# Two small transfers per attention job begun from ScalarE's queue instead of SyncE's, in a two-layer transformer kernel

## The chip, the cores and the metric

The kernel runs on one core of one Trainium2 chip. The time is device microseconds (us) of one execution of the whole program, and of several runs the median is taken. Engines are named as in the profile: PE is TensorE (PEld its weight loads), ACT is ScalarE, DVE is VectorE, POOL is GpSimd and SP is SyncE. SP does no arithmetic in this kernel: it begins the transfers.

## The reference

The input `x` has shape (2, 1024, 1024) in float32. Four blocks follow one another, each of the form `x = x + block(layernorm(x))`:

1. causal attention with rotary positions, 32 query heads and 8 key/value heads of width 32, over 2 sequences of 1024 tokens;
2. a mixing block: per token a 4x4 matrix made doubly stochastic in 50 Sinkhorn iterations, which mixes four streams of 256 columns, and one small matmul branch;
3. a second causal attention of the same sizes with the other pairing of the rotary columns;
4. a linear layer of 1024 by 1024 with a bias plus a mixture of eight rank-16 adapters, whose weights come from a softmax gate and a threshold.

For the change only the attention matters. For one group of 4 query heads that share a key head:

```python
scores = q @ k.T / sqrt(32)          # masked above the diagonal
attn = softmax(scores, axis=-1)      # minus the row's maximum inside the exponential
out = attn @ v
```

## The kernel before

**Tiles and stages.** Tokens are taken in blocks of 512. Matmuls are done in three passes on pairs of a high and a low part (`PASSES`), so that float32 accuracy is kept. The plan `P0 P1 O0 M0 P2 O1 ...` (`PLAN`) orders the dense work of both layers: P projects a block to queries, keys and values, O is the output projection, M the logits of the mixing block, F the last linear layer with its mixture. Beside it run the attention jobs: 8 blocks by 8 key heads are 64 jobs (`JOBS`), counted here from 0 to 63. PE's work is dealt out from six streams: results, values, branches, scores, maxima and the dense rest.

**One attention job.** `load_job` brings keys into a tile `kst` and the four heads' queries into a tile `qst` (rows 0 to 95 of its partitions; three of each rotate). Then come three passes over the same scores:

- `maxima_of` computes the scores with queries on the partitions (L1002). DVE takes the row's maximum, with its sign turned, into a column of `nm` (L1012), and ACT makes the sum of the exponentials (L1027, an ACTIVATE and a read of its accumulator). That is 16 rows of tiles per job. At the end PE transposes `nm` into a bank (L1039), and DVE writes the transposed row of maxima into `lt` as a high part (`lt[:, 0]`, L1045) and a low part (`lt[:, 1]`, L1050).
- Two small transfers (L1055 to L1063) copy `lt[:, 0]` and `lt[:, 1]`, 8 KB each, into partitions 96 and 97 of `qst`. Rows 96 and 97 of `kst` hold ones, so the next matmul subtracts the maxima by itself.
- `scores_of` computes the scores again, with keys on the partitions and these two more rows (L1091). ACT takes the exponential out of the bank into `pt` (L1098), POOL masks the diagonal (L1108), and `values_of` multiplies by the values (L1154).

The event `summed[j]` stands for the landing of both small transfers, and the first matmul of L1091 of job j waits for it.

**What sets the order.** Nothing is ordered by the compiler: a planner written in the kernel (`Planner`) plays the program through with costs for every operation and writes the instructions out in the order in which it begins them. An operation's `fn` is called at its planned beginning. So each engine runs its own instructions in that order, and the places of instructions of different engines in the one written list tell what the planner held to be simultaneous. Transfers are planned by `pl.dma` on SP: 430 ns of SP for each, and eight "lanes" in turn: a transfer waits until the transfer eight before it in the list has landed, since both count on one semaphore. Which engine really begins a transfer is decided by what `fn` calls: everywhere in this kernel `nc.sync.dma_start`. The planner's cost for a transfer stays with SP whatever `fn` calls.

An engine's queue is strictly in order. An instruction that waits for a semaphore holds up all that stand behind it on the same engine.

Of the kernel before, what the change touches and what calls it, by code (L numbers as in the profile page):

```python
# [66 lines left out]
def fp(ap):  # L67
    return ap.bitcast(FP)
# [3 lines left out]
def t_act(n, sbuf=False, accum=False):  # L72
    ns = n / 1.2 + (95.0 if sbuf else 66.0)
    if accum:
        ns += 170.0
    return max(ns, 95.0), max(ns, 95.0) + 105.0


def t_dve(n):
    return n / 0.96 + 67.0, n / 0.96 + 150.0  # L80
# [15 lines left out]
def t_pe(n):  # L96

    return max(n, 256) * 0.4531 + 2.0
# [408 lines left out]
def kernel(ctx: ExitStack, tc: tile.TileContext, a: dict, out: bass.AP):  # L507
    nc = tc.nc
# [469 lines left out]
    def maxima():  # L978
        for j, (n, g) in enumerate(JOBS):
            yield from maxima_of(j, n, g)  # L980

    def maxima_of(j, n, g):

        half = n % 2
        kt, qt, _, there, _ = loaded[j]


        npc = half + 1
        nm, nm_was, nm_rel = nm_ring.take()
        ds, ds_was, ds_rel = ds_ring.take()  # L990
        found, sums = [], []
        for i in range(TPB):
            N = (half * TPB + i + 1) * P // npc
            M = max(N, 256)
            for r in (0, 2, 1, 3):
                col = slice(r * 4 + i, r * 4 + i + 1)
                ms, ms_was, ms_rel = ms_ring.take()
                ev = None
                for p in range(npc):

                    def go(bk, r=r, i=i, p=p):
                        nc.tensor.matmul(  # L1002
                            bk[:, :M], qt[0:96, r, i * P : (i + 1) * P],
                            kt[0:96, p * N : p * N + M], start=True, stop=True,
                        )

                    end, bank = yield Step(
                        [there], t_pe(M), go, bank=True, quota=of_sums
                    )

                    def least(sc=bank.tile[:, :N], col=col, N=N, p=p, ms=ms):
                        nc.vector.tensor_tensor_reduce(  # L1012
                            out=ms[:, p * N : (p + 1) * N], in0=sc,
                            in1=cmask[:, TB - N :] if p == half else zero.to_broadcast([P, N]), scale=1.0,
                            scalar=nm[:, 1, col] if p else MASKED,
                            op0=ALU.add, op1=ALU.min, accum_out=nm[:, int(p < half), col],
                        )

                    ev = pl.dve(
                        (N / 0.96 + 142.0, N / 0.96 + 225.0), least,  # L1020
                        [end, nm_was, ms_was] + ([ev] if ev else []), PRI_SUMS,
                    )
                    bank.free.follow(ev)
                found.append(ev)
                ev = pl.act(
                    t_act(npc * N, True, accum=True),
                    lambda ms=ms, col=col, N=N: nc.scalar.activation(  # L1027
                        ms[:, : npc * N], ms[:, : npc * N], AF.Exp, bias=nm[:, 0, col], scale=-1.0,
                        accum_out=ds[:, col],
                    ),  # L1030
                    [ev, ds_was], PRI_DEN,
                )
                ms_rel.follow(ev)
                sums.append(ev)

        ev = pl.dve((175.0, 265.0), lambda ds=ds: nc.vector.reciprocal(ds, ds), sums)
        dens[j] = (ds, ev, ds_rel)
        end, bank = yield Step(
            found, T_TURN, lambda bk, nm=nm: nc.tensor.transpose(bk[:16, :P], nm[:, 0], ident), bank=True  # L1039
        )  # L1040
        nm_rel.follow(end, *sums)
        lt, was, rel = lt_ring.take()
        tp = bank.tile[:16, :P]
        ev = pl.dve(
            t_dve(P), lambda lt=lt, tp=tp: nc.vector.tensor_scalar(lt[:, 0], tp, -1.0, None, ALU.mult),  # L1045
            [end, was], PRI_SUMS,
        )
        ev = pl.dve(
            t_dve(P),
            lambda lt=lt, tp=tp: nc.vector.scalar_tensor_tensor(  # L1050
                lt[:, 1], tp, -1.0, fp(lt[:, 0]), ALU.mult, ALU.subtract
            ), [ev], PRI_SUMS,
        )
        bank.free.follow(ev)
        evs = [  # L1055
            pl.dma(
                512,
                lambda q=q, qt=qt, lt=lt: nc.sync.dma_start(
                    fp(qt[96 + q : 97 + q]).rearrange("k r q -> k (r q)"), fp(lt[:, q])
                ), 16, [ev], -2,  # L1060
            )
            for q in range(2)
        ]  # L1063
        rel.follow(*evs)
        summed[j].follow(*evs)
# [873 lines left out]
```

## Time and profile before

| what | value |
|---|---|
| three runs of the kernel | 2308.69, 2311.53, 2321.01 us; median 2311.53 |
| the profiled execution | 2316.82 us, of which its span (first to last instruction) is 2315.1 us |
| granted TensorE clock | 0.991 of full speed |
| PE, DVE, ACT, POOL busy | 97%, 79%, 73%, 43% of the span |
| instructions that ACT executes | 4062 |
| transfers begun by SP | 1363, of which 128 are those of the change |

How to read the profile: "busy" is the time in which an engine executes; waiting, and the beginning of a transfer, are not counted. The ends of matmuls are modelled, so a busy PE can still be held up a little. "SPq" is SyncE's sequencer, which begins transfers. In a line of the timeline the columns are start in us, duration in us, engine, line of the program, operation, output<-inputs with their shapes and a count; brackets show idle time of the engine just before and what ended it. In a line of waits the columns are who waited for whom, the total in us, how often, and the longest.

### The profile page before, as it was taken

How to read it: one execution, taken by the hardware profiler on the slowest of the kernel's cores; microseconds unless marked ns; L12 is line 12 of the kernel's file. 1: busy time of each engine (PE TensorE's matmuls, PEld its weight loads, DVE VectorE, ACT ScalarE, POOL GpSimd, SP SyncE). 2: the span in 40 equal slices, each digit the busy share in tenths (PEclk: the TensorE clock that was granted, in tenths of full speed). 3: DMA queues.
4: the chain of work that ended last, by engine and by line, in shares of the span. 5: the costliest groups of instructions: out<-in, count | busy, mean ns of one | idle time of the engine just before them, and what ended most of it. 6: DMA issues, size and time to landing. Idle time of an engine off the chain costs nothing.

```text
span 2315.1 us, 42175 instructions
## 1 busy us (share of the span) xinstructions
PE 2244.4 (97%) x12544; PEld 1639.6 (71%) x12544; DVE 1834.3 (79%) x5826; ACT 1697.5 (73%) x4062; POOL 992.3 (43%) x1438
## 2 busy tenths in 40 slices
PE   9999999999999999999999999999999999999999
PEld 8767856666676766667776676668777766666787
DVE  7767979998898999988899989978875887656253
ACT  4798769999574899999978867862894697558320
POOL 5444424555456654325763345643443423212100
PEclk9999999999999999999999999999999999999999
DMA  8866554447667655438683565448857826453554
GB/s 295 275 182 216 198 173 138 141 134 238 211 214 242 210 160 189 141 102 271 191 260 112 170 224 184 142 167 288 287 164 247 274 83 223 132 184 94 209 190 146
DMA packets 217750, 445.69 MB, mean 193 GB/s; under 512 B 55984, under 2 KB 66480, under 8 KB 211376
## 3 DMA queue, kind: packets, MB, share of 16 engines
q1 hardware_dynamic: 217520, 442.99, 59.1%
q8 instruction: 99, 1.62, 0.3%
q14 instruction: 131, 1.07, 0.1%
HBM read 308.16 MB, written 133.69 MB: 191 GB/s over the span
## 4 chain that ended last, share of the span: by engine, by line
PE 73%; DVE 10%; DMA 9%; ACT 4%; issue 2%; POOL 1%; SPq 1%; DVEq 0%; POOLq 0%; ACTq 0%
PE bank L859 16%; PE bank L1275 13%; PE bank L1002 11%; PE bank L1091 9%; PE bank L1154 9%; PE bank L1716 8%; DVE ms L1012 3%; PE bank L816 3%; DMA qst<-qd 2%; ACT ms L1027 2%; ACT pt L1098 2%; DMA qst<-lt 1%; PE bank L783 1%; DMA x<-x 1%; DVE stat L737 1%
## 5 line engine op out<-in xcount | busy, mean ns | idle before, releaser
L1027 ACT ACTIVATE ms<-ms,nm 128x128 f32<-128x128 f32 (+5 forms) x1024 | 802.4, 791 | 77.0 <-DVE nm L1012 74.8
L1098 ACT ACTIVATE pt<-bank 128x512 f32<-128x512 f32 (+1 forms) x1216 | 657.6, 592 | 98.6 <-PE bank L1091 95.2
L1002 PE MATMUL bank<-kst,qst 96*128 96x384 f32 (+4 forms) x1536 | 494.2, 367 | 23.1 <-DMA qst<-qd 15.6
L859 PE MATMUL bank<-zT,w 128*128 128x512 f32 x1920 | 504.6, 397 | 0.0
L1091 PE MATMUL bank<-qst,kst 98*128 98x512 f32 (+1 forms) x1216 | 430.6, 400 | 17.9 <-DMA qst<-lt 8.6
L1275 PE MATMUL bank<-w,zT 128*128 128x512 f32 x1536 | 413.6, 398 | 4.8 <-DMA zT<-od 2.2
L859 PEld LDWEIGHTS bank<-zT,w 128*128 128x128 f32 x1920 | 354.9, 189 | 81.5 <-issue 8.6
L1002 PEld LDWEIGHTS bank<-kst,qst 96*128 96x128 f32 x1536 | 276.2, 191 | 180.9 <-DVE nm L1012 34.5
L1108 POOL TENSOR_SCALAR_AFFINE_SELECT pt<-pt 128x256 f32<-128x256 f32 (+1 forms) x448 | 208.5, 469 | 369.6 <-ACT pt L1098 364.5
L1012 DVE CUSTOM_DVE_ANT_0 ms<-bank,cmask,nm 128x448 f32<-128x448 f32 (+3 forms) x512 | 316.9, 628 | 29.5 <-PE bank L1002 12.8
L1275 PEld LDWEIGHTS bank<-w,zT 128*128 128x128 f32 x1536 | 284.7, 189 | 66.8 <-issue 4.9
L1012 DVE CUSTOM_DVE_ANT_0 ms<-bank,zero 128x448 f32<-128x448 f32 (+3 forms) x512 | 292.6, 577 | 45.8 <-PE bank L1002 33.8
L1154 PE MATMUL bank<-pt,vst 128*32 128x512 f32 (+3 forms) x3072 | 315.5, 497 | 2.9 <-POOL pt L1108 1.6
L1091 PEld LDWEIGHTS bank<-qst,kst 98*128 98x128 f32 x1216 | 224.5, 190 | 96.4 <-issue 23.9
L660 POOL TENSOR_TENSOR w<-rw,w 128x512 fp32r<-128x512 f32 x169 | 224.7, 1330 | 150.8 <-ACT w L651 119.8
L1012 DVE CUSTOM_DVE_ANT_0 ms<-bank,cmask 128x384 f32<-128x384 f32 (+3 forms) x512 | 234.4, 480 | 51.6 <-ACT ms L1027 34.1
L651 ACT CAST w<-rw 128x512 fp32r<-128x512 f32 x156 | 97.1, 623 | 182.0 <-DMA rw<-in_w 69.9
L1027 ACT ACTIVATION_READ_ACCUMULATOR ms<-ms,nm 128x1 f32 x1024 | 216.9, 212 | 0.0
L1716 PE MATMUL bank<-w,zT 128*128 128x512 f32 x768 | 194.9, 398 | 0.0
L1154 PEld LDWEIGHTS bank<-pt,vst 128*32 128x32 f32 x3072 | 76.6, 108 | 134.2 <-issue 86.2
L1716 PEld LDWEIGHTS bank<-w,zT 128*128 128x128 f32 x768 | 143.6, 189 | 37.1 <-issue 4.8
L659 DVE TENSOR_TENSOR w<-rw,w 128x512 fp32r<-128x512 f32 x77 | 61.9, 804 | 85.0 <-ACT w L651 82.0
(171 smaller groups left out, 2812.7 us busy)
## 6 DMA issues: line engine op xcount, KB each, us to landing
rw<-in_w SPq DMA_DIRECT2D x246, 256.0 KB, 3.3
w<-wd SPq DMA_DIRECT2D x114, 512.0 KB, 4.3
x<-x SPq DMA_DIRECT2D x72, 512.0 KB, 5.0
qd<-st SPq DMA_DIRECT2D x64, 512.0 KB, 4.3
qst<-qd SPq DMA_DIRECT2D x64, 512.0 KB, 5.9
od<-st SPq DMA_DIRECT2D x63, 512.0 KB, 3.6
zT<-od SPq DMA_DIRECT2D x63, 512.0 KB, 8.1
wd<-w SPq DMA_DIRECT2D x38, 512.0 KB, 4.0
```

What stands on the lines that cost most here:

```text
L651: (ACT, t_act(512, True), lambda: nc.scalar.copy(me.tile[:, 0], raw)),
L660: (GPS, t_gtt(512), lambda: nc.gpsimd.tensor_tensor(me.tile[:, 1], raw, fp(me.tile[:, 0]), ALU.subtract), True),
L859: nc.tensor.matmul(ps, w.tile[:, i, (c % 4) * P : (c % 4 + 1) * P], zT[:, j, c, :], start=(c == 0 and m == 0), stop=(c == NC - 1 and m == 2),)
L1002: nc.tensor.matmul(bk[:, :M], qt[0:96, r, i * P : (i + 1) * P], kt[0:96, p * N : p * N + M], start=True, stop=True,)
L1012: nc.vector.tensor_tensor_reduce(out=ms[:, p * N : (p + 1) * N], in0=sc, in1=cmask[:, TB - N :] if p == half else zero.to_broadcast([P, N] ...
L1027: lambda ms=ms, col=col, N=N: nc.scalar.activation(ms[:, : npc * N], ms[:, : npc * N], AF.Exp, bias=nm[:, 0, col], scale=-1.0, accum_out=d ...
L1091: nc.tensor.matmul(to, ks, qs, start=True, stop=True)
L1098: lambda to=pt[:, r : r + nm], st=bank.tile, nm=nm, W=W: nc.scalar.activation(to, st[:, : nm * W].rearrange("p (r t) -> p r t", r=nm), AF. ...
L1108: lambda pt=pt, nh=nh: nc.gpsimd.affine_select(out=pt[:, :, :P], in_=pt[:, :, :P], compare_op=ALU.is_ge, fill=0.0, base=0, pattern=[[0, nh ...
L1154: nc.tensor.matmul(to[HD * r : HD * r + HD, q0:], vt[:, kb, :], pts[r * len(pts) // 4][0][:, r % (4 // len(pts)), :], start=(kb == 0), sto ...
L1275: nc.tensor.matmul(ps, zT[:, x, c, i * P : (i + 1) * P], ws[c].tile[:, y, :], start=(c == 0 and m == 0), stop=(c == NC - 1 and m == 2),)
L1716: nc.tensor.matmul(ps, x_, w_, start=(c == 0 and m == 0), stop=(c == NC and m == 2))
```

## The change

The two small transfers of the row of maxima are begun by ACT on its own queue, `nc.scalar.dma_start` in place of `nc.sync.dma_start`. The planner is not told: it goes on planning them on SP, so the written list keeps its order, and no other instruction is added, removed or moved.

```diff
@@ -1055,7 +1055,7 @@
         evs = [
             pl.dma(
                 512,
-                lambda q=q, qt=qt, lt=lt: nc.sync.dma_start(
+                lambda q=q, qt=qt, lt=lt: nc.scalar.dma_start(
                     fp(qt[96 + q : 97 + q]).rearrange("k r q -> k (r q)"), fp(lt[:, q])
                 ), 16, [ev], -2,
             )
```

## The prediction

> **What bounds the kernel now.** I read the page first, then the waits, the view of the tile `lt`, the chain, and the timeline around single jobs.
>
> ```profile
> PE 2244.4 (97%) x12544; PEld 1639.6 (71%) x12544; DVE 1834.3 (79%) x5826; ACT 1697.5 (73%) x4062; POOL 992.3 (43%) x1438
> ...
> PE 73%; DVE 10%; DMA 9%; ACT 4%; issue 2%; POOL 1%; SPq 1%; DVEq 0%; POOLq 0%; ACTq 0%
> ```
>
> PE is busy nearly throughout: only 2315.1 - 2244.4 = 70.7 us of the span are PE idle, and all that the change could win on PE is among them. ACT's 73% is a mean, and the stretches differ:
>
> ```profile
> 410.00:550.00 140.00, 140.00 (x806) 93.91 (x805) 127.19 (x470) 135.09 (x324) 81.84 (x141) 1.00 0.45 142
> 550.00:660.00 110.00, 105.28 (x617) 77.94 (x616) 94.19 (x259) 73.78 (x209) 50.11 (x62) 1.00 0.79 262
> ```
>
> After the stretch and its length stand PE, PEld, DVE and ACT busy. From 410 to 550 us ACT is busy 135 of 140 us; from 550 to 660 only 74 of 110. New work on ACT is nearly free in the second and not in the first. Of the small transfers the view of `lt` and the waits say:
>
> ```profile
> L1058 SPq DMA_DIRECT2D qst<-lt x128: 503/525/1861, 85.0 to 2121.8; - x128
> ...
> DMA to landing us min/median/max: 1.8/2.9/11.8
> ```
>
> ```profile
> PE bank L1002 <- DMA qst<-qd: 15.6, 8, 4.0
> PE bank L1091 <- DMA qst<-lt: 8.6, 6, 2.8
> ...
> PE bank L1091 <- ACT pt L1098: 4.4, 8, 1.2
> ```
>
> SP spends 525 ns (median) beginning one; it lands 1.8 to 11.8 us later. PE idles for them 8.6 us in all, in 6 jobs of 64; all 8.6 us may be won, hardly more.
>
> **Removed from SP.** 128 beginnings of 0.525 us, 67 us of SP, and the waits for DVE ahead of them. That matters where a transfer right behind them ends on the chain. I went through the six transfers behind each pair: of the 33 transfers on the chain six stand there, in an unbroken row (the first after job 7, 27, 46, 53, 55, 58). Each can start up to 1.05 us sooner: 0 to -6.3 us. I take **-3**.
>
> **Added to ACT: the beginnings.** 128 x 0.525 = 67.2 us, 1.05 us a job, as no row shows a transfer begun by ACT. From below: semaphore instructions on ACT's sequencer take 17 ns (rows of L1027) and end, in the median, 0.34 us before the end of an ACTIVATE in front of them, so the sequencer runs ahead and may hide part. Behind a read of the accumulator, which most of the 64 places follow, they end with it, so there it hides nothing. From above: 1.86 us each, SP's maximum. I take 0.85 us a job, near the 1.05 of SP's rows, with 0.4 and 1.05 as ends.
>
> How much reaches PE? In the written list I took the place of each pair, and from the ACT instruction behind it followed the recorded waits (ACT's own order, ACT to DVE, POOL and PE, with some 35 to 75 ns per hand-over) to the first matmul; the smallest sum of the gaps is how late ACT may be there without PE being late. The easiest place to read is job 29:
>
> ```profile
> 952.21 1.16 SPq L1058 DMA_DIRECT2D qst<-lt  x2
> ...
> 953.66 0.29 ACT L1027 ACTIVATION_READ_ACCUMULATOR ms<-ms,nm 128x1 f32 x1
> 953.75 0.96 ACT L1098 ACTIVATE pt<-bank 128x384 f32<-128x384 f32 x2
> ...
> 954.38 0.19 PEld L1091 LDWEIGHTS bank<-qst,kst 98*128 98x128 f32 x1
> 954.47 0.35 PE L1091 MATMUL bank<-qst,kst 98*128 98x384 f32 x1
> ```
>
> SP begins at 952.21. ACT reaches the place, between the two ACT rows, at 953.95; then comes the exponential, whose first half ends at 954.33, and PE's next weights load at 954.38, 0.05 us later, into the bank it empties. The allowance is zero; 0.85 us there is 0.85 us for PE. In job 61 the allowance is 7 us. Over 64 jobs, 38 have less than 0.85 us; the shortfalls sum to **24.2 us** (8.4 us at a delay of 0.4, 32.0 at 1.05).
>
> **Added to ACT: waits.** The pair now waits on ACT for `lt` (DVE L1045, L1050) and for the landing of the transfer eight before. Against ACT's recorded arrival DVE is mostly done (median 0.7 us earlier) and the lane free. Exceptions, such as jobs 43 (4.1 us, lane), 1 (1.7), 56 (2.1) and 20 (1.4), sum to 13.1 us. Behind the waiting transfer stand the exponentials of L1027 and L1098, for which DVE (`ms`), POOL (`pt`) and PE (banks) wait. The share that passes on I take as above, 24.2 of 54.4: **+5.8**.
>
> Both make 30 us. PE's other idle time, 70.7 - 8.6 = 62 us or 1 us a job, is partly spent waiting for things that ACT doesn't delay, and eats some lateness. I take off a fifth: **+24**.
>
> **Moved: when the pair lands.** The second is begun 1.25 us later than on SP (mean over jobs: ACT arrives later, and in 45 jobs has one to six instructions between the two). Yet a transfer on ACT's queue doesn't stand behind SP's. In the trace 24 of 64 land in under 1.9 us, and those behind a backlog take longest, as job 56's second:
>
> ```profile
> 1828.28 4.02 SPq L1255 DMA_DIRECT2D zT<-od  x7
> ...
> 1835.65 2.30 SPq L1058 DMA_DIRECT2D qst<-lt  x2
> ```
>
> Behind seven loads of 512 KB it took 10.4 us. At 1.8 us throughout, PE saves 8.9 us of its gaps and is late by 2.7 in ten jobs (-6.2). At 2.9, now's median, it saves 8.4 and loses 20.0 (+11.6). Some sharing remains; I take 2.1 us: 8.9 saved, 5.8 lost, **-3**.
>
> [...]
>
> **Sum.** -3 + 24 - 3 = +18 us. Against the profiled execution that is 2316.8 + 18 = 2335 us; that run lay 5.3 us above the median of three, so against the median 2311.5 + 18, rounded to **2330 us**. 0.5% is 11.6 us, about what a measurement of this kernel can tell from no change.
>
> **Rivals.**
>
> *It is hidden (about 2313).* The sequencer runs ahead and ACT loses 0.4 us a job: 8.4 + 3 for waits, less 6.2 for landing at 1.8 us and 3 for SP, +2. For it: ACT's median of 0.34 us ahead, and that PE idles for ACT only 4.4 us now. Against it: PE's weight loads do wait for ACT, 22.0 us in 32 cases (L1002) and 20.4 in 46 (L1091).
>
> *Faster (about 2297): the transfers leave SP's backlog.* The chain runs through `qst<-lt` five times (6.9, 5.3, 3.1, 3.4, 10.4: 29.1 us). At 1.8 us each, 20 us go; SP's part gives 6 more; less 8.4 + 3 on ACT, -15. It decides if ACT loses under some 0.4 us a job and landing takes 1.8 us. Against it: PE's idle before those matmuls is 8.6 us, so not all 20 can come out.
>
> *ACT becomes the bound (about 2385).* All 67 us plus 13 us of waits pass on, less 6 as above. For it: long rows without ACT gaps, such as 1891 to 1907 us. Against it: ACT idles 27% overall.
>
> *It does not do what it says:* ACT's transfers land as slowly as SP's; then the landing term is +11.6 and the time 2344, within the forecast's range.
>
> **How the numbers follow.** Forecast (2316 to 2350) 0.50, of which 0.37 lies over 0.5% slower and 0.13 within; hidden 0.20, of which 0.17 within and 0.03 slower; faster 0.18; ACT the bound 0.12. So faster 0.18, same 0.17 + 0.13 = 0.30, slower 0.37 + 0.03 + 0.12 = 0.52. The range from 2299 to 2368 leaves out about half of the faster case (0.09) and most of the last (0.09).
>
> **What would show it.** Beginnings: rows of L1058 on ACT, near 0.5 us, ACT idle before the instruction behind them. Passing on: PEld waits for ACT (L1002, L1091) above 22.0 and 20.4 us, PE idle above 70.7. Landing: a median near 2.1 us and the 8.6 us wait of L1091 nearly gone. I am wrong if ACT's rows of L1058 are far from 0.5 us, if PE's idle time doesn't grow, or if most new PE idle is behind transfers that SP begins.

## The result and the profile after

The changed kernel takes 2335.49 us (median of 6 runs, 2331.26 to 2347.62), the kernel before in the same setting 2312.67 us (6 runs, 2307.27 to 2321.01). The ratio is 1.0104, with a 95% interval from 1.0082 to 1.0125: about 24 us slower. The profiled execution of the changed kernel took 2336.56 us with a span of 2334.8 us, 19.7 us more than that of before.

The same two lines of the page as shown of before, busy times and the chain, now read:

```profile
PE 2253.0 (96%) x12544; PEld 1639.3 (70%) x12544; DVE 1831.5 (78%) x5826; ACT 1697.8 (73%) x4062; POOL 996.5 (43%) x1438
...
PE 75%; DMA 9%; DVE 8%; ACT 3%; issue 2%; POOL 1%; SPq 1%; ACTq 0%; DVEq 0%; POOLq 0%
```

PE is idle for 2334.8 - 2253.0 = 81.8 us instead of 70.7, which is 11.1 of the 19.7 us. The other 8.6 us are matmuls that took longer. ACT's busy time has not moved (1697.8 us against 1697.5), since beginning a transfer isn't counted as busy. The tile `lt`, again with the rows that answer to those of before:

```profile
L1058 ACTq DMA_DIRECT2D qst<-lt x128: 510/516/1583, 82.7 to 2139.6; - x128
...
DMA to landing us min/median/max: 1.8/2.7/7.9
```

A beginning on ACT takes 516 ns in the median, as on SP (525), and the landing takes 2.7 us, hardly less than 2.9. PE's waits, columns as before:

```profile
PE bank L1002 <- DMA qst<-qd: 10.7, 5, 4.0
PE bank L1002 <- DVE nm L1012: 9.9, 12, 3.0
PE bank L1091 <- DVE nm L1012: 5.9, 9, 1.8
PE bank L1002 <- ACT rd L1222: 5.2, 1, 5.2
PE bank L1091 <- ACT pt L1098: 4.6, 8, 1.4
...
PE bank L1091 <- DMA qst<-lt: 3.3, 3, 1.4
```

The two rows of before on DVE's maxima (`nm`):

```profile
PE bank L1002 <- DVE nm L1012: 4.6, 7, 1.4
...
PE bank L1091 <- DVE nm L1012: 1.9, 5, 0.7
```

The wait for the pair itself is nearly gone (8.6 to 3.3 us). What is new is PE waiting for DVE's maxima (4.6 to 9.9 us at L1002, 1.9 to 5.9 at L1091) and one wait of 5.2 us for ACT's `rd`. DVE did not become slower (1831.5 us busy, 1834.3 before). It was held up by ACT, as ACT's own waits say:

```profile
ACT ms L1027 <- DMA od<-st: 7.2, 2, 3.7
...
ACT ms L1027 <- DMA zT<-od: 5.7, 2, 4.3
ACT rd L1222 <- DMA kst<-kd: 5.6, 1, 5.6
ACT ms L1027 <- DMA qst<-qd: 5.0, 1, 5.0
```

None of these four lines exists before. They look absurd: the sum of exponentials at L1027 has nothing to do with the output `od`, with its reload `zT` or with another job's queries. The timeline resolves it. Here is ACT at job 56:

```profile
1848.09 0.83 ACT L1027 ACTIVATE ms<-ms,nm 128x640 f32<-128x640 f32 x1
1848.82 0.19 ACT L1027 ACTIVATION_READ_ACCUMULATOR ms<-ms,nm 128x1 f32 x1
1852.65 0.52 ACTq L1058 DMA_DIRECT2D qst<-lt  x1
1853.27 0.83 ACT L1027 ACTIVATE ms<-ms,nm 128x640 f32<-128x640 f32 x1 [4.26 <-DMA zT<-od]
...
1859.43 0.52 ACTq L1058 DMA_DIRECT2D qst<-lt  x1
1860.05 0.83 ACT L1027 ACTIVATE ms<-ms,nm 128x640 f32<-128x640 f32 x1 [5.04 <-DMA qst<-qd]
```

ACT stands still from 1849.01 to 1852.65 although DVE had written the first half of `lt` by 1846.00, and starts nothing that stands behind the small transfer; in both traces its 4062 instructions start in the same order. The waiting instruction is the small transfer, and it waits for its lane: the transfer eight before it in the list has to land, since both count on one semaphore. For the first that is the sixth of seven loads `zT<-od` of 512 KB (begun 1843.68, landed 1852.63), for the second a load `qst<-qd` (begun 1847.22, landed 1859.41); each of the two begins 0.02 us after that landing. SP had only just begun them, behind megabytes of other loads (the first row holds the last five of the seven loads):

```profile
1842.15 3.21 SPq L1255 DMA_DIRECT2D zT<-od  x5
...
1847.22 0.50 SPq L952 DMA_DIRECT2D qst<-qd  x1
```

Such stalls stand in four jobs: 5.57 us in job 1, 1.39 and 3.56 in job 18, 3.68 and 1.67 in job 43, 4.26 and 5.04 in job 56, **25.2 us of ACT's time in all**. Of these, 20.7 us are the wait for the lane. The other 4.5 us are the seven beginnings behind these waits: there ACT has nothing left to do, so a beginning stands in the open, some 0.6 us each up to ACT's next row (1852.65 to 1853.27). I compared matmul by matmul when PE starts it after and before. PE falls behind by 6.25 us from 550 to 660 us (job 18), 7.4 from 1320 to 1430 (job 43) and 5.6 from 1760 to 1880 (job 56), together 19.2 of the 19.7 us. Job 1 leaves 1.5 us, because PE's old wait of 2.85 us for its pair goes. What the other stretches add and give back nearly cancels.

**Why these places.** With all transfers on SP, the eighth before a transfer is also eight back in SP's own queue, usually long landed (for the small transfers in the trace of before, 9.4 us earlier in the median, under 0.1 us earlier for 8 of the 128). Once two engines begin transfers, the lanes are still dealt in the one written list into which the framework merges all engines: in the trace of after ACT's 128 transfers count on the same eight semaphores as SP's 1235. The planner's list kept its order; this merged list did not, which the semaphores of the transfers' landings show. In it the pair now stands later among SP's transfers than it did: by 3 and 3 places in job 1, by 2 and 5 in job 18, by 6 and 7 in job 43, by 3 and 6 in job 56, and by none for 87 of the 128. "Eight before" then means one that SP began a few us ago. The ACT instructions behind the pair make `ms`, whose tiles DVE needs back for L1012, and PE waits for DVE: that is the chain behind the lines above.

### The profile page after: what moved, and what is told of

Read it like the earlier page. It is cut to its first block, busy times and chain, and to the rows that moved or that the text cites. A ratio compares the mean times of both kernels' runs of the same rounds, so it can differ in the third digit from the quotient of the medians.

```text
span 2334.8 us, 42125 instructions
## 1 busy us (share of the span) xinstructions
PE 2253.0 (96%) x12544; PEld 1639.3 (70%) x12544; DVE 1831.5 (78%) x5826; ACT 1697.8 (73%) x4062; POOL 996.5 (43%) x1438
## 4 chain that ended last, share of the span: by engine, by line
PE 75%; DMA 9%; DVE 8%; ACT 3%; issue 2%; POOL 1%; SPq 1%; ACTq 0%; DVEq 0%; POOLq 0%
PE bank L859 17%; PE bank L1275 13%; PE bank L1002 11%; PE bank L1091 9%; PE bank L1154 9%; PE bank L1716 8%; DMA qst<-qd 3%; PE bank L816 3%; DVE ms L1012 2%; DMA x<-x 1%; ACT pt L1098 1%; DVE stat L737 1%; PE bank L783 1%; ACT ms L1027 1%; DMA zT<-od 1%
## 5 line engine op out<-in xcount | busy, mean ns | idle before, releaser
L1027 ACT ACTIVATE ms<-ms,nm 128x128 f32<-128x128 f32 (+5 forms) x1024 | 801.7, 790 | 93.4 <-DVE nm L1012 70.9
L1098 ACT ACTIVATE pt<-bank 128x512 f32<-128x512 f32 (+1 forms) x1216 | 657.8, 591 | 96.5 <-PE bank L1091 91.3
L1002 PE MATMUL bank<-kst,qst 96*128 96x384 f32 (+4 forms) x1536 | 498.0, 369 | 30.8 <-DMA qst<-qd 10.7
L1091 PE MATMUL bank<-qst,kst 98*128 98x512 f32 (+1 forms) x1216 | 432.8, 401 | 20.4 <-DVE nm L1012 5.9
L1002 PEld LDWEIGHTS bank<-kst,qst 96*128 96x128 f32 x1536 | 276.8, 191 | 194.5 <-DVE nm L1012 44.3
L859 PEld LDWEIGHTS bank<-zT,w 128*128 128x128 f32 x1920 | 354.8, 189 | 81.8 <-issue 8.6
L1012 DVE CUSTOM_DVE_ANT_0 ms<-bank,cmask,nm 128x448 f32<-128x448 f32 (+3 forms) x512 | 317.1, 629 | 25.7 <-PE bank L1002 9.3
L1012 DVE CUSTOM_DVE_ANT_0 ms<-bank,zero 128x448 f32<-128x448 f32 (+3 forms) x512 | 293.0, 578 | 53.1 <-PE bank L1002 28.0
L1091 PEld LDWEIGHTS bank<-qst,kst 98*128 98x128 f32 x1216 | 225.7, 191 | 101.8 <-ACT pt L1098 21.0
L1012 DVE CUSTOM_DVE_ANT_0 ms<-bank,cmask 128x384 f32<-128x384 f32 (+3 forms) x512 | 234.6, 480 | 57.9 <-ACT ms L1027 39.4
L1027 ACT ACTIVATION_READ_ACCUMULATOR ms<-ms,nm 128x1 f32 x1024 | 215.5, 210 | 0.0
```

What stands on the lines that cost most here:

```text
L859: nc.tensor.matmul(ps, w.tile[:, i, (c % 4) * P : (c % 4 + 1) * P], zT[:, j, c, :], start=(c == 0 and m == 0), stop=(c == NC - 1 and m == 2),)
L1002: nc.tensor.matmul(bk[:, :M], qt[0:96, r, i * P : (i + 1) * P], kt[0:96, p * N : p * N + M], start=True, stop=True,)
L1012: nc.vector.tensor_tensor_reduce(out=ms[:, p * N : (p + 1) * N], in0=sc, in1=cmask[:, TB - N :] if p == half else zero.to_broadcast([P, N] ...
L1027: lambda ms=ms, col=col, N=N: nc.scalar.activation(ms[:, : npc * N], ms[:, : npc * N], AF.Exp, bias=nm[:, 0, col], scale=-1.0, accum_out=d ...
L1091: nc.tensor.matmul(to, ks, qs, start=True, stop=True)
L1098: lambda to=pt[:, r : r + nm], st=bank.tile, nm=nm, W=W: nc.scalar.activation(to, st[:, : nm * W].rearrange("p (r t) -> p r t", r=nm), AF. ...
```

## The experiments

Each was timed in several rounds beside the kernel before on the same chip. That kernel's median differs between chips (2313.1, 2317.6 and 2317.9 us in the three groups of runs), so ratios are compared; a difference in us is the ratio times the median of its group. Each profile is of one execution, which can lie up to some 11 us from its kernel's median (e4: 2325.2 against 2336.7 us).

**1 and 2. The four jobs alone, and all others.** In e1 the pairs of jobs 1, 18, 43 and 56 go back to SP, all others stay on ACT:

```diff
-                lambda q=q, qt=qt, lt=lt: nc.scalar.dma_start(
+                lambda q=q, qt=qt, lt=lt, j=j: (nc.sync if j in (1, 18, 43, 56) else nc.scalar).dma_start(
```

In e2 the two engines in that line are exchanged, so that only those four are on ACT.

> The pairs of jobs 1, 18, 43 and 56 are begun by SyncE as before, the other 60 pairs by ScalarE. Theory 'lane' (ScalarE loses its time in these four jobs, where it waits for the landing of a transfer of SyncE that counts on the same semaphore): the loss is gone, within 5 us of the kernel before, ScalarE idle at the 60 places about as long as before. Rival 'issue' (the recorded prediction's main term: 0.5 us of ScalarE for each beginning, spread over some 38 jobs): 60 of 64 pairs keep their cost, +21 us. Rival 'late landing' (the second transfer of every pair begins later): +15 to +20 us.

> Only the pairs of jobs 1, 18, 43 and 56 are begun by ScalarE, the other 60 by SyncE. 'Lane': most of the change's loss, +14 to +22 us, with ScalarE idle 3 to 6 us at these places and TensorE idle there. 'Issue': 8 beginnings of 0.5 us, at most +4 us. 'Late landing': +1 to +2 us.

e1: ratio 1.0026 [1.0006, 1.0047], or +6.0 us for 60 jobs. e2: 1.0069 [1.0047, 1.0092], or +16.0 us for 4 jobs. For e1 that is a little outside the 5 us of 'lane', but far from the 15 to 21 us of the rivals; e2 is as 'lane' said. The two add up to 22 of the 24 us. So 120 of the 128 moved transfers cost about a quarter of the loss and 8 cost two thirds. In e2's profile PE falls behind by 5.75, 5.76 and 5.60 us in the stretches of jobs 18, 43 and 56, and ACT's four odd waits are all there; in e1's they are gone.

**3 and 5. The other merge.** A switch of the framework's context decides how the engines' lists are merged into the one in which lanes are dealt. Each engine's own order is the same in both. With the other rule, the pairs of those four jobs stand no later among SP's transfers than before. (In e3 some pairs of other jobs stand up to four places later, but ACT shows no long wait there: L1027, L1098 and L1222 wait for transfers once, 1.2 us. By this, a later place cost ACT time only in the four jobs, where SP had a backlog.) e3 has all 64 pairs on ACT, e5 only the four.

```diff
-    with tile.TileContext(nc, schedule_with_timeline_sim=True) as tc:
+    with tile.TileContext(nc, schedule_with_timeline_sim=False) as tc:
```

> All 64 pairs on ScalarE as in the change, every engine's order unchanged; only the order in which the engines' instructions are merged into one list differs, and with it which transfer stands eight before each one, that is which landing a transfer waits for. The four jobs' pairs no longer have a transfer that SyncE has only just begun as their predecessor, some twenty other second transfers have one that is two to four places younger. 'Lane': most of the loss goes, 0 to +9 us. 'Issue' and 'late landing': unchanged, +20 to +25 us.

> Only the pairs of jobs 1, 18, 43 and 56 are begun by ACT, and the written list is merged by the other rule, under which every engine keeps its order and no pair is dealt a later lane. Theory 'lane' (the loss is ACT's wait for a transfer that SP has only just begun): the 18.6 us that these four jobs cost under the first merge are gone; between -7 us (jobs 1 and 56 no longer stand behind SP's backlog) and +2 us against before, and no ACT idle time above 1 us behind a transfer of these four jobs. Rival 'issue' (each beginning costs ACT its 0.5 us): +1.5 us, and it cannot be told from the lane theory by the time alone, but then ACT's instruction behind each pair starts some 0.5 to 1 us later than in before. Rival 'the place': in these four jobs any transfer begun by ACT is dear, whatever lane it has: +15 to +19 us, as with these four under the first merge.

e3: 1.0000 [0.9979, 1.0020]. The whole loss of the change is gone with all 128 transfers still on ACT. e5: 0.9971 [0.9955, 0.9988], 6.7 us *faster* than before, where the same four jobs under the first merge cost 16.0. The rival "the place" is out. Where the 6.7 us come from is shown less firmly, since no run has the other merge with all transfers on SP. In e5's profile PE waits 3.5 us for the pairs, against 8.6 before:

```profile
PE bank L1091 <- DMA qst<-lt: 3.5, 3, 1.6
```

ACT at job 56 in e5:

```profile
1837.13 0.59 ACT L1222 COPY rd<-bank 128x512 f32<-128x512 f32 x1
1837.27 0.53 ACTq L1058 DMA_DIRECT2D qst<-lt  x1
1837.62 0.83 ACT L1027 ACTIVATE ms<-ms,nm 128x640 f32<-128x640 f32 x1
1838.35 0.19 ACT L1027 ACTIVATION_READ_ACCUMULATOR ms<-ms,nm 128x1 f32 x1
1838.44 0.82 ACT L1027 ACTIVATE ms<-ms,nm 128x640 f32<-128x640 f32 x1
1839.16 0.19 ACT L1027 ACTIVATION_READ_ACCUMULATOR ms<-ms,nm 128x1 f32 x1
1839.22 0.51 ACTq L1058 DMA_DIRECT2D qst<-lt  x1
1839.25 0.82 ACT L1027 ACTIVATE ms<-ms,nm 128x640 f32<-128x640 f32 x1
```

The same two transfers are begun while the instruction ahead of them still runs, and the row behind starts without a gap (1837.62, 1839.25).

**4. Another engine.** All pairs are begun by GpSimd (`nc.gpsimd` in the same line).

> All 64 pairs are begun by GpSimd, whose transfers count on semaphores of their own, so no pair waits for a transfer of SyncE. 'Lane': no engine waits for a landing of SyncE's at these places; what is lost is GpSimd's own time for the beginnings, perhaps 1 us each, on an engine that is busy 43%: 0 to +15 us. 'Issue' (an engine pays for each beginning, and GpSimd has more room than ScalarE): 0 to +10 us. It tells the two apart only by the traces: whether long waits at the four jobs remain.

1.0096 [1.0066, 1.0125], +22 us, above both ranges that I gave. The 1 us that I allowed for a beginning was an estimate that no run shows; in e4 one takes 547 ns in the median, and the view of `lt` names no transfer that POOL waited for there. The waits of POOL and of PE:

```profile
POOL qst L1058 <- DVE lt L1045: 44.3, 9, 18.2
```

```profile
PE bank L1091 <- DMA qst<-lt: 13.2, 9, 3.1
```

POOL reaches the place early and stands there 44.3 us for DVE, and PE's wait for the pairs grows from 8.6 to 13.2 us. None of ACT's four odd waits is there, so the loss has another cause. Which one is open: the longer wait of PE for the pairs is 4.6 of the 22 us, and the profiled execution was the fastest of the nine. The run says nothing for or against the lanes.

**6. The wait alone.** All transfers on SP. At the eight places ACT copies one element, which depends on the same landing (or on the tile's release by it) that the changed kernel's ACT waited for. No part of the computation is changed.

```diff
+    BACK = {(1, 0): 5, (1, 1): 4, (18, 0): 6, (18, 1): 2, (43, 0): 2, (43, 1): 1, (56, 0): 5, (56, 1): 1}
...
+            t, s = [x for x in begun if x not in pairs][-back]
+            if "od" in t.tensor.name:
+                nc.scalar.copy(first(s), junk[0:1, :])
+            else:
+                nc.scalar.copy(junk[0:1, :], first(t))
+        begin(to, src)
```

> All 128 small transfers are begun by SP as before. In jobs 1, 18, 43 and 56 ACT is given, at the eight places at which it began a transfer in the changed kernel, a copy of one element that depends on the landing (or on the tile's release) of the very transfer that the changed kernel's ACT waited for; the added work on ACT is eight copies of one element, under 0.3 us each, and one memset on DVE. Theory 'lane': the wait alone makes the loss: +12 to +20 us, with ACT idle 3 to 6 us in each of the four jobs. Rivals 'issue' and 'late landing' (the cost is in beginning the transfer on ACT, or in where its data lands): at most +2 us, since neither is there.

1.0051 [1.0032, 1.0070], +11.8 us. The size is just under the lower end that I gave, and far above the 2 us of the rivals. The view of the tile `junk` shows what the eight copies waited for:

```profile
  DMA od<-st: 6.6, 2
  DMA zT<-od: 6.6, 3
  DMA qst<-qd: 4.3, 1
  DMA kst<-kd: 3.6, 1
```

That is 21.1 us of ACT's time, as long as the 20.7 us of lane waits in the changed kernel. What e6 leaves out is the 4.5 us of beginnings in the open behind them, and it costs 4.2 us less than e2 (11.8 against 16.0); the two figures agree, though the intervals of e2 and e6 overlap. PE falls behind by 5.6, 4.3 and 4.8 us in the three stretches. So a wait for these landings is enough to make a loss of this kind, with no transfer begun on ACT.

**7 and 8. The time of the beginnings as real work.** All transfers on SP. At each of the 128 places ACT makes a copy within a tile of its own: of 128x340 elements in e7, of one element in e8.

```diff
-                lambda q=q, qt=qt, lt=lt: nc.sync.dma_start(
+                lambda q=q, qt=qt, lt=lt: nc.scalar.copy(junk, junk) and nc.sync.dma_start(
```

> All pairs are begun by SP as before; at each of the 128 places where the changed kernel's ACT begins a transfer, ACT makes one copy of 128x340 two-byte elements within its own tile, which nobody waits for and which waits for nobody: an estimated 0.35 to 0.5 us each, 0.7 to 1.0 us a job (estimated from the copies of 128x256 that took 0.38 to 0.39 us and those of 128x512 that took 0.59). It gives ACT the time that the prediction charged for the beginnings (0.85 us a job) as real work. If the prediction's table of allowances holds (24.2 us at 0.85 us a job, 32.0 at 1.05, a fifth taken off): +14 to +25 us, and the failed step of the prediction is the price of a beginning alone. If PE's slack takes it up, the table itself was wrong: under +8 us.

> As the run before it, but each copy is of a single element: 0.19 us each by the single-element copies of the run with the waits alone, 0.38 us a job. By the table of allowances (8.4 us at 0.4 us a job, a fifth off): +4 to +9 us. If PE's slack takes it up: -1 to +3 us.

e7: 1.0068 [1.0045, 1.0091], +15.8 us. A copy took 476 ns; copies overlap their neighbours, and ACT's busy time grew by 1742.0 - 1697.5 = 44.5 us, 0.70 us a job. e8: 1.0004 [0.9991, 1.0016], +0.9 us. That is below what I expected by the table, and within the -1 to +3 us that I gave for PE's slack taking it up; a copy took 177 ns, but ACT's busy time grew by 9.8 us only, 0.15 us a job. The gap is closed only by a reading made after the result: my table of allowances, read between its entries, gives 18.9 us at 0.70 us a job and 3.2 at 0.15 (on the line from zero to 8.4 at 0.4). Less the fifth that is 15.1 and 2.5 us, and both lie in the measured intervals. It is e7 that supports the table, since e8's interval also holds zero. Real work on ACT also shows where I had said, in PEld's waits:

```profile
PEld bank L1091 <- ACT pt L1098: 28.2, 70, 1.7
```

Before it was 20.4 us in 46 cases, in the changed kernel 21.0 in 46.

**9. What the other pairs cost.** The other merge, with the pairs of nine jobs on SP: those at which PE waited for the pair in the runs with most pairs on ACT.

```diff
-                lambda q=q, qt=qt, lt=lt: nc.scalar.dma_start(
+                lambda q=q, qt=qt, lt=lt, j=j: (nc.sync if j in (4, 6, 7, 8, 15, 26, 37, 48, 55) else nc.scalar).dma_start(
```

> The list merged by the other rule, with the pairs of the nine jobs 4, 6, 7, 8, 15, 26, 37, 48 and 55 on SP and those of the other 55 on ACT. These nine are the ones before whose L1091 PE waited for the pair in the runs with most pairs on ACT, job 1 apart. With all 64 on ACT under this merge the time was that of before, with four only it was 0.29% less. Theory 'late landing' (what is left of the loss is that the second transfer is begun later and lands later, where PE needs it at once): -3 to -7 us, PE's wait of L1091 for qst<-lt at 3 to 5 us instead of 8.5. Rival 'beginnings' (the rest of the loss is ACT's own time for so many beginnings): -1 to +2 us, as with all 64.

0.9972 [0.9956, 0.9988], -6.5 us: with 55 of the 64 pairs on ACT the time is that of e5 with four, as "late landing" has it. PE's wait in e3, then in e9:

```profile
PE bank L1091 <- DMA qst<-lt: 8.5, 8, 1.8
```

```profile
PE bank L1091 <- DMA qst<-lt: 4.6, 5, 1.7
```

3.9 of the 6.5 us between e3 and e9 are in this line. The intervals of e3 and e9 just overlap, and they ran on different chips: this step is supported, less firmly than the others. e5 and e9 are the versions that beat both kernels, each a little less than 0.3% under the kernel before.

## Why the prediction came out right in its number and wrong in its split

The forecast was 2330 us, the median is 2335.5: +18 us by the sum, +24 by the ratio, +19.7 between the two profiles. The sign holds and the size nearly, but they come from another term than the one I gave them to. That the sum came out near is luck: one term was far too large, another far too small, and the two errors nearly cancel.

**Beginnings on ACT, 24.2 us before the fifth is taken off: this step failed.** It is near nothing. I wrote that behind a read of the accumulator the sequencer hides nothing, and charged 0.85 us a job. The trace of after shows the transfer begun, in the median, 0.4 us before the instruction ahead of it ends, and at the 62 places behind a read of the accumulator 0.42 us before that read ends. At the 104 places with one transfer between two ACT instructions, the time from the start of the one to the start of the other grew by a median of 0.00 us. The sum of 31.5 us there is nearly all the lane waits: in e3, without them, it is 5 us. The places with both transfers between two ACT instructions add 3.5 us in e3, so all 128 cost ACT some 8 us where I had charged 64 x 0.85 = 54.4. Job 29, my example of an allowance of zero, is the plainest. ACT after:

```profile
956.34 1.24 ACT L1027 ACTIVATE ms<-ms,nm 128x1024 f32<-128x1024 f32 x1
956.54 0.55 ACTq L1058 DMA_DIRECT2D qst<-lt  x1
957.38 0.28 ACT L1027 ACTIVATION_READ_ACCUMULATOR ms<-ms,nm 128x1 f32 x1
957.47 0.96 ACT L1098 ACTIVATE pt<-bank 128x384 f32<-128x384 f32 x2
```

The transfer is begun inside the ACTIVATE, and the exponential starts 0.09 us after the read starts, exactly as in the rows of before (953.66 and 953.75). The table of allowances itself holds where e7 tests it: 0.70 us of real work a job costs 15.8 us. The price put into it was wrong. Accordingly PEld's waits for ACT, which I had said would rise above 22.0 and 20.4 us, are 21.9 and 21.0.

**Waits on ACT, 5.8 us: the mechanism was right, the size wrong.** I worked out 13.1 us of waits, with jobs 43, 1 and 56 among the exceptions and job 18 not. There were 25.2 us in four jobs; in the profile PE falls 19.2 us behind in three of them, and alone (e2) the four cost 16.0 us. I also let 44% of a wait reach PE (24.2 of 54.4 us); in e2 it was 16.0 of 26.2 us. And the sum held PE's busy time fixed at 2244.4 us; it grew by 8.6 us, in part by a lower granted clock (0.989 of full speed against 0.991; last section). The step that failed is the place in the list: I took "the transfer eight before" from SP's old order, and the merge had moved the pair. My last sentence on what would prove me wrong, new PE idle time behind transfers that SP begins, has come true by way of ACT.

**Landing at 2.1 us, -3 us: wrong in the median, and small.** 2.7 us after, and 3.0 in e3: the landing stays nearly where it was (2.9). The 2.1 us were my choice between 1.8 and 2.9 us, and no run shows them. In the trace of after 95 of the 128 begin while other transfers are on their way, and land after 3.6 us in the median (before: 102, 3.3 us); the other 33 land after 1.8 (before: 26, 1.8). That a transfer on ACT's queue doesn't stand behind SP's shows in 17 of the 128, which land ahead of a transfer that SP began earlier; before, none did. And PE gains in e5, which is 6.7 us faster: it waits 3.5 us for the pairs instead of 8.6. In the other jobs the second transfer, begun later, takes about as much back (e1 and e3 against e9).

**SP freed, -3 us:** no run isolates it; if it exists, it is within the gains of e5 and e9.

**The rivals.** *Hidden* was right on its main point, that ACT loses next to nothing to the beginnings, and e3, without the lane waits, takes 2313.95 us, the time of before on that chip (2313.1). *Faster* names a gain that exists, of 6.7 us rather than 15, and that shows only without the lane waits. *ACT the bound* is out. *Doesn't do what it says* was right on the landing (2.7 us after, 2.9 before).

## What to carry to other kernels

Before moving a transfer to another engine's queue, find the semaphore on which it will count and which transfer has to land before it may start, in the list after the change and not in that of before. Here the beginning itself was nearly free on a busy engine (a median delay of 0.00 us), while one wait for somebody else's load stopped everything behind it on ACT, for up to 5.57 us. And a sum that comes out right proves none of its terms: it took experiments on single terms to see that one was near zero and another some three times too small.

## What the runs showed that I had not expected

**An idle PE was paid for twice.** After the stall at job 56, in stretches of 4 us of the changed kernel (stretch, length, PE, PEld, DVE, ACT, POOL busy, then granted clock, DMA share, GB/s):

```profile
1856.00:1860.00 4.00, 2.61 (x12) 1.83 (x10) 0.68 (x4) 0.00 (x0) 0.00 (x0) 1.00 0.99 225
1860.00:1864.00 4.00, 1.83 (x6) 1.05 (x6) 2.71 (x9) 3.95 (x9) 0.00 (x0) 0.97 0.92 349
1864.00:1868.00 4.00, 3.94 (x9) 2.95 (x10) 3.56 (x13) 3.65 (x8) 0.00 (x0) 0.50 0.02 7
1868.00:1872.00 4.00, 4.00 (x18) 2.54 (x17) 2.27 (x7) 3.24 (x8) 0.00 (x0) 0.68 0.01 2
1872.00:1876.00 4.00, 4.00 (x23) 2.94 (x16) 3.55 (x12) 3.68 (x8) 0.00 (x0) 1.00 0.00 0
```

PE is busy for 4.4 of 8 us, and then is granted half its clock for 6.83 us (1863.76 to 1870.59), of which it is busy 6.54. Summed as (1 - granted clock) x time over rows of 2 us, the stretches of jobs 18, 43 and 56 lose 3.4, 6.8 and 3.4 us to the clock after, and 0, 3.4 and 0 before: 10.3 us more. PE's idle time in them grew by 7.6 us. So between these two profiles more than half of the 19.2 us is not the wait but the clock after it. The other runs say how firm that is: in the three profiles with the waits (after, e2, e6) these stretches lose 10.2 to 13.6 us to the clock, in the eight others 1.7 to 6.8. Over the whole span the clock took 25.6 us after and 21.5 before, since before had such spells elsewhere; in e3's profile it took 9.6 us, so one profiled execution can lie several us from its kernel's median. PE's longest single idle time around the stall at job 56 was 3.01 us:

```profile
1861.62 0.47 PE L1002 MATMUL bank<-kst,qst 96*128 96x448 f32 x1 [3.01 <-DVE nm L1012]
```

In the 4 us before each of the ten half-rate spells of this trace PE was busy for 1.47 to 2.64 us, and before the one at 361.9 us its longest single idle time was 1.04 us. An idle time of 3.32 us that ends at 1974.70 has no such spell behind it: the granted clock stays at 1.00 up to 1986 us. So the rows show that the spells follow idle time, but not which idle time brings one on.

**ACT began transfers while it computed.** In the changed kernel the 516 ns of its sequencer are mostly hidden behind arithmetic (0.4 us ahead in the median, and in the median no delay behind), except where ACT has already run dry in front of the transfer. On GpSimd (e4) a beginning takes 547 ns in the median and counts as busy time of the engine: POOL went from 992.3 to 1055.4 us.
